# Two softmax attentions whose q and k are projected densely and laid to row quadrants by transfers, with the row maxima as a ninth row, halved weighted sums, and FP4 blocks three at a time

## The chip, the cores and the metric

The kernel runs on one core of one Trainium2 chip. A core has five engines that run side by side and wait for one another by semaphores: TensorE (PE, matrix products; loading its weights is listed apart as PEld), VectorE (DVE), ScalarE (ACT), GpSimd (POOL) and SyncE (SP, which issues transfers). PE writes to PSUM only. The metric is the device time of one execution, in microseconds.

## The reference, cut to what matters

The model is a chain of four layers, each of the form feed-forward, attention, feed-forward. The activations are 4 batches of 1024 tokens of width 128, all in float32. The change touches the feed-forward and the attention of layer 0, the attention of layer 1, and one detail of the expert layers.

- Layer 0, feed-forward (run before and after its attention): inputs and weights are quantized to FP4 in blocks of 16 values (scale = largest magnitude / 6), then gate and up projections of width 352, silu times up, quantized again, and a down projection.
- Layer 0, attention: 16 heads of 8, **causal**, softmax, then an output projection, a recurrence of 8 steps with tanh, and a dense feed-forward with gelu.
- Layer 1, attention: 16 heads of 8, **not causal**, with biases.

```python
qkv = (xn @ qkv_w + qkv_b).reshape(b, s, 3, H, HD)
scores = jnp.einsum('bhqd,bhkd->bhqk', q, k) / np.sqrt(HD)
attn_w = jax.nn.softmax(scores, axis=-1)
attn = jnp.einsum('bhqk,bhkd->bhqd', attn_w, v)
```

Layers 2 and 3 (experts, two linear attentions, ternary feed-forwards) are not touched, but for the expert layers' scatter.

## The kernel before

Tokens are cut into 8 blocks of 512 (two to a batch), which stay in SBUF as `x`. Every stage is a Python generator; each `yield` is a point where another generator may put its instructions into the engines' queues. `run` advances the stage of the moment and gives each of its steps one `tick` to the side queue, in which the start of the next batch, the end of the last batch and the front of the next stage wait. `woven` runs several generators in turn. The tile framework places the instructions, adds the semaphores and finds free buffers; each engine then executes its own queue strictly in order.

**Attention (lines 552 to 717).** The 16 heads are taken in 4 groups of 4 (`NG`), for each of 4 batches: 16 groups an attention, counted `n`. PE's 128 rows are used as four quadrants of 32 rows: head `i` of a group has its 8 values of q and k in rows `32i` to `32i+7`, and the weights are padded with zeros to bring them there (`_packed_heads`). Two chains run for each group:

- `maxima` first projects q and k of the group (L591, two matmuls of 128x512 for each half of the 1024 tokens; the profile has two records for every f32 matmul), evicts them with their biases (L594 on ACT, L595 on DVE), then computes scores with queries in the partitions (L607) and reduces them over the keys on DVE, negated (L619). In the causal case a mask is added by a matmul of bf16 (L613). At the end of a group the maxima are transposed (L385) and added to q as a ninth row (L627, `qm`). That k has a one in its ninth row makes the next scores come out with the maximum subtracted.
- `weighted` computes the scores again with keys in the partitions (L653), takes the exponential on ACT (L658), masks the diagonal on POOL when causal (L661), and sums the values weighted by it (L640, four heads in four column groups of 32, so that `acc` gets 4 x 32 rows). Values carry a column of ones, so the sum of weights comes along. The sums of one chunk of keys are issued after the scores of the next. When 512 queries are done, `acc` is copied (L672), transposed, and divided by the sum of the weights (L676, L677).

`softmax_attention` weaves both: each step of `weighted` (two heads of one chunk of 128 keys) is followed by one step of the maxima of the next group; weighting of a group begins `LEAD = 4` steps after its maxima are complete. A step of the weaving is below called half a step where a whole one is a chunk of keys for four heads. Scores, accumulators and transposes share the pool `ps_one` of four PSUM buffers of 2 KB a partition; `big` has two buffers of 4 KB, for maxima and projections.

**FP4 feed-forward (lines 499 to 549).** `l0_block` handles one block of 512 tokens: layernorm, quantization (`fp4`, a chain over DVE and POOL, L460 to L473), transposes, projections (L524), silu and product, quantization again, transposes, down projection (L541) into an `acc` that the block holds from its first projection to its end. Two blocks are woven, 12 steps apart. When the second FP4 stage begins, the last batch of the attention's end (output projection, recurrence L824 and L825, gelu feed-forward) still runs from the side queue, and blocks 6 and 7 need it.

**Expert layers.** `front` routes the tokens of a chunk of blocks and scatters their rows to DRAM with indirect transfers from POOL (L1321), two for each tile of 128 tokens, with a yield after every second tile.

Of the kernel before, what the change touches and what calls it, by code (L numbers as in the profile page):

```python
# [46 lines left out]
LEAD = 4  # L47
# [3 lines left out]


def _packed_heads(w, extra=None):

    out = np.zeros((*w.shape[:-1], 32), np.float32)
    out[..., :HD] = w
    if extra is not None:
        out[..., HD] = extra
    return out
# [7 lines left out]
def _softmax_attn_weights(q, k, v, out_w, bq, bk, bv, out_b):  # L67

    ws = [
        _packed_heads(q).reshape(D, H * 32),  # L70
        _packed_heads(k).reshape(D, H * 32),
        v.reshape(D, D),
        out_w,
    ]
    vecs = [
        _columns(_packed_heads(bq).reshape(-1)),

        _columns(_packed_heads(bk, 1.0).reshape(-1)),
        _columns(out_b),
    ]  # L80
    return np.concatenate(ws, 1), np.concatenate(vecs, 1), np.tile(bv.reshape(1, D), (P, 1))
# [123 lines left out]
class _Kernel:  # L205
# [5 lines left out]
    def __init__(self, ctx, tc, ins, out):  # L211
# [3 lines left out]
        self.mix = ctx.enter_context(tc.tile_pool(name="mix", bufs=2))  # L215

# [213 lines left out]
    def opened(self, name, side):  # L430

        stack = ExitStack()
        pool = stack.enter_context(self.tc.tile_pool(name=name, bufs=2, side=side, reuse_waits="tile"))

        def close():
            stack.close()
            return
            yield

        return pool, close  # L440
# [60 lines left out]
    def l0_ffn(self, side):  # L501
        pool, close = self.opened("l0f", side)
        done = self.follow
        yield from woven((self.l0_block(pool, blk, done) for blk in range(NBLK)), 2, 12)
        finish(close())
# [46 lines left out]
    def attention_tiles(self, pool):  # L552

        self.mxs = [pool.tile([P, NT, 4, 32], F32, tag=f"mx{k}", name=f"mx{k}", bufs=1) for k in range(2)]
        for t in self.mxs:
            self.nc.gpsimd.memset(t, 0.0)
        self.vas = [pool.tile([P, NT, VW], F32, tag=f"va{k}", name=f"va{k}", bufs=1) for k in range(2)]
        for t in self.vas:
# [21 lines left out]
    def maxima(self, pool, out, mx, xnT, g, wqk, vecs, causal):  # L580

        nc = self.nc
        qT = pool.tile([P, S], F32, tag="qT", name="qT", bufs=2)
        kT = pool.tile([P, S], F32, tag="kT", name="kT", bufs=3)
        for half in range(S // BLK):
            cols = bass.ts(half, BLK)
            ps = self.big()
            for j in range(2):  # L590
                nc.tensor.matmul(  # L591
                    ps[:, j, :], lhsT=wqk[:, bass.ts(j * NG + g, P)], rhs=xnT[:, cols], start=True, stop=True
                )
            nc.scalar.activation(qT[:, cols], ps[:, 0, :], AF.Identity, bias=vecs[:, g : g + 1])  # L594
            nc.vector.tensor_scalar(kT[:, cols], ps[:, 1, :], vecs[:, NG + g : NG + g + 1], None, ALU.add)  # L595
        part = pool.tile([P, NT, 2, 4], F32, tag="part", name="part", bufs=2)
        for t in range(NT):
            n = (t + 1) * P if causal else S
            for c in range(0, n, BLK):
                w = min(n - c, BLK)  # L600
                diag = causal and c + w == n
                for pair in range(2):
                    heads = (2 * pair, 2 * pair + 1)
                    ps = self.big()
                    for j, i in enumerate(heads):
                        rows = slice(32 * i, 32 * i + 32)
                        nc.tensor.matmul(  # L607
                            ps[:, j, :w], lhsT=qT[rows, bass.ts(t, P)], rhs=kT[rows, c : c + w],
# [7 lines left out]
                    to = part[:, t, c // BLK, 2 * pair : 2 * pair + 2]  # L616
                    if n <= BLK:
                        to = mx[:, t, 2 * pair : 2 * pair + 2, HD]
                    nc.vector.tensor_reduce(to, ps[:, :, :w], AX.X, ALU.max, negate=True)  # L619
                    yield  # L620
        first = TPB if causal else 0
# [841 lines left out]
```

## Time and profile before

| what | time |
|---|---|
| median of 3 runs | 5242.22 us (5237.9 to 5248.3) |
| the profiled execution | 5245.33 us |
| its span, first to last instruction | 5243.6 us |
| mean granted TensorE clock | 0.893 |
| busy: PE, DVE, ACT, POOL | 4429.8, 2539.3, 1714.6, 1040.5 us |

By start and end of the lines named, the stages are: first FP4 feed-forward to about 235 us; causal attention from there to 1286, when its last accumulator is copied; second FP4 feed-forward, with the end of the last batch, to 1623; routing and experts of layer 1; attention of layer 1 from 1979 to 3265; the rest, which the change leaves alone, to 5243.6. PE's busy time covers matmuls whose ends are modelled and which overlap, so it is not a measure of how full the array is. What an engine waits for is put down to the last semaphore that released it.

### The profile page before, as it was taken

The page shows a single profiled execution, that of the slowest core. Times are in us where ns is not written, and L with a number is a line of the kernel's source. Part 1 is how long each engine was busy: PE and PEld are TensorE (multiplying, and loading weights), DVE is VectorE, ACT ScalarE, POOL GpSimd, SP SyncE. Part 2 cuts the span into 40 slices and gives each one's busy share as a digit, 9 for nine tenths or more (in the row PEclk, how much of TensorE's full clock was granted, in tenths as well). Part 3 has the DMA queues.
Part 4 walks back from the last instruction along what each step waited for, and adds up shares of the span by engine and source line. Part 5 has one row for each costly group of instructions (what it writes and reads, how often), then busy time and mean ns, then how long its engine had stood idle before and what let it go on. Part 6 is the DMA issues. An engine that isn't in the chain of part 4 may idle for free. (4 is left out here: it accounts for less than half of the span.)

```text
span 5243.6 us, 51536 instructions
## 1 busy us (share of the span) xinstructions
PE 4429.8 (84%) x19588; PEld 1969.4 (38%) x19588; DVE 2539.3 (48%) x5415; ACT 1714.6 (33%) x3016; POOL 1040.5 (20%) x1403
## 2 busy tenths in 40 slices
PE   4799999998743987999988998695596859699899
PEld 3533333333432442333333332342243534244544
DVE  8666766573853336666655663333313721321510
ACT  1134443443211221554544545121232423122322
POOL 4211111111343014000010010104514241500000
PEclk8699999998865996999999999897797879799999
DMA  2000000000000320000000000231132013100000
GB/s 88 0 1 1 1 1 1 1 1 1 1 16 36 118 96 29 1 1 1 1 12 5 1 13 1 94 115 60 35 134 77 34 66 137 44 0 0 1 8 8
DMA packets 68090, 162.91 MB, mean 31 GB/s; under 512 B 13739, under 2 KB 22443, under 8 KB 67075
## 3 DMA queue, kind: packets, MB, share of 16 engines
q0 software_dynamic: 29632, 93.89, 5.3%
q1 hardware_dynamic: 38211, 65.73, 3.7%
q8 instruction: 155, 2.54, 0.2%
q14 instruction: 92, 0.75, 0.0%
HBM read 110.54 MB, written 49.02 MB: 30 GB/s over the span
## 5 line engine op out<-in xcount | busy, mean ns | idle before, releaser
L658 ACT ACTIVATE es<-sc 128x512 f32<-128x512 f32 (+3 forms) x1792 | 883.3, 553 | 976.2 <-PE sc L653 588.9
L653 PE MATMUL sc<-qm,kT 32*128 32x512 f32 (+3 forms) x3584 | 1090.4, 602 | 19.1 <-ACT es L658 17.6
L619 DVE TENSOR_REDUCE part<-big 128x2 f32<-128x1024 f32 (+3 forms) x768 | 880.9, 1156 | 432.6 <-PE big L607 299.5
L607 PE MATMUL big<-kT,qT 32*128 32x512 f32 (+3 forms) x3584 | 1015.9, 630 | 41.6 <-DVE part L619 27.3
L653 PEld LDWEIGHTS sc<-qm,kT 32*128 32x128 f32 x3584 | 380.9, 188 | 653.4 <-ACT es L658 398.7
L1355 PE MATMUL big<-xT,w 128*128 128x512 f32 x1104 | 520.7, 602 | 2.7 <-ACT xT L1406 2.7
L372 POOL TENSOR_TENSOR ln_rs<-ln_ve,neg_half 128x4 f32<-128x4 f32 x120 | 126.7, 1057 | 1665.2 <-DVE ln_ve L371 1661.4
L1207 PE MATMUL big<-h,l3f_w 128*128 128x512 f32 x1024 | 445.6, 596 | 4.6 <-DVE h L1193 3.2
L640 PE MATMUL acc<-es,va 128*32 128x512 f32 (+3 forms) x3584 | 446.7, 578 | 2.4 <-issue 2.3
L607 PEld LDWEIGHTS big<-kT,qT 32*128 32x128 f32 x3584 | 297.2, 193 | 177.2 <-DVE part L619 103.2
L1348 PE MATMUL acc<-h,w 128*128 128x512 f32 x736 | 361.2, 593 | 1.1 <-DVE h L1359 1.1
L1355 PEld LDWEIGHTS big<-xT,w 128*128 128x128 f32 x1104 | 209.3, 193 | 250.0 <-issue 245.7
L661 POOL TENSOR_SCALAR_AFFINE_SELECT es<-es 128x128 f32<-128x128 f32 x512 | 162.5, 327 | 702.7 <-ACT es L658 694.1
L1321 POOL DMA_INDIRECT rows_in<-xn,rows x256 | 248.8, 972 | 261.3 <-DVE p_to L1010 140.0
L1207 PEld LDWEIGHTS big<-h,l3f_w 128*128 128x128 f32 x1024 | 194.4, 191 | 251.1 <-issue 241.7
L1039 POOL DMA_INDIRECT y<-rows_out,rows x256 | 250.9, 980 | 188.7 <-DMA rows_out<-yr 88.6
L1359 DVE TENSOR_TENSOR h<-h,big 128x512 f32<-128x512 f32 x184 | 126.6, 688 | 319.3 <-ACT h L1358 319.3
L375 DVE TENSOR_SCALAR xn<-x,ln_mv,ln_rs 128x128 f32<-128x128 f32 x352 | 115.8, 380 | 308.7 <-PE tr L385 108.6
L385 PE MATMUL tr<-ident,fp_q 128*88 128x128 f32 (+1 forms) x324 | 74.8, 395 | 185.1 <-POOL fp_q L473 185.1
L1358 ACT ACTIVATE h<-big 128x512 f32<-128x512 f32 x184 | 109.9, 597 | 324.8 <-PE big L1355 324.8
L1363 ACT ACTIVATE h<-big 128x1024 f32<-128x1024 f32 x124 | 126.9, 1024 | 246.7 <-PE big L1355 193.7
L385 PE MATMUL tr<-ident,xn 128*128 128x128 f32 x288 | 59.9, 329 | 165.7 <-issue 115.6
(277 smaller groups left out, 5038.9 us busy)
## 6 DMA issues: line engine op xcount, KB each, us to landing
xr<-rows_in SPq DMA_DIRECT2D x92, 256.0 KB, 2.6
rows_out<-yr SPq DMA_DIRECT2D x92, 256.0 KB, 2.0
rows_in<-zero SPq DMA_DIRECT2D x5, 1024.0 KB, 7.6
rows_in<-xn,rows POOLq DMA_INDIRECT x256
y<-rows_out,rows POOLq DMA_INDIRECT x256
l3f_w<-in_l3f_w SPq DMA_DIRECT2D x1, 2816.0 KB
x<-in_x SPq DMA_DIRECT2D x8, 256.0 KB, 5.9
out<-x SPq DMA_DIRECT2D x8, 256.0 KB, 2.3
```

The costliest lines, as they stand in the source:

```text
L385: self.nc.tensor.transpose(ps[:n, i * P : (i + 1) * P], t, self.ident)
L607: nc.tensor.matmul(ps[:, j, :w], lhsT=qT[rows, bass.ts(t, P)], rhs=kT[rows, c : c + w], start=True, stop=not diag,)
L619: nc.vector.tensor_reduce(to, ps[:, :, :w], AX.X, ALU.max, negate=True)
L640: nc.tensor.matmul(out[32 * i : 32 * i + 32, off:], lhsT=va[:, kc, (4 * g + i) * (HD + 1) :][:, :32], rhs=es[i][:, off:], start=kc == 0, s ...
L653: nc.tensor.matmul(ps[:, off:], lhsT=kT[rows, bass.ts(kc, P)], rhs=qm[rows, qb * BLK + off : (qb + 1) * BLK], start=True, stop=True,)
L658: nc.scalar.activation(es[i][:, off:], ps[:, off:], AF.Exp, scale=ISQ)
L661: nc.gpsimd.affine_select(out=block, in_=block, compare_op=ALU.is_ge, fill=0.0, base=0, pattern=[[1, P]], channel_multiplier=-1,)
L1039: nc.gpsimd.indirect_dma_start(out=y, out_offset=None, in_=self.rows_out[:, :], in_offset=bass.IndirectOffsetOnAxis(ap=rows[:, k, t : t + ...
L1207: nc.tensor.matmul(ps[:, j, :], lhsT=m[:, i * FF + (2 * pair + j) * P : i * FF + (2 * pair + j + 1) * P], rhs=hs[z][:, i, :], start=i == 0 ...
L1321: put = nc.gpsimd.indirect_dma_start(out=k.rows_in[:, :], out_offset=bass.IndirectOffsetOnAxis(ap=self.rows[:, i, first + t : first + t + ...
L1348: nc.tensor.matmul(out, lhsT=w[:, (2 if gated else 1) * FF + c * D :][:, :D], rhs=h, start=c == 0, stop=c == NC - 1)
L1355: nc.tensor.matmul(ps[:, j, :], lhsT=w[:, bass.ts(col, P)], rhs=xT, start=True, stop=True)
```

## The change

Dense projection: the weights of q and k are no longer padded. `dense` projects all 16 heads of a batch at once (two matmuls of 128x512 for each half), and `laid_out` copies, for each group, the 8 partitions of each head's q and k to a quadrant with four transfers on SP, into one of three tiles `qks`, a group ahead of its maxima. `qks` was filled with ones, so that row 8 of k is one.

Maxima: they are finished for each half of the queries; one transpose brings the 4 heads x 4 tiles to 16 rows, which are copied, written to DRAM and read back as four rows of 512, each to row 8 of q in its quadrant. `maxima` contracts 8 rows, the second scores 9. Weighting of a half starts 6 steps after its maxima (`LEAD`).

Sums: `summed` cuts the sums of a chunk into two halves of 256 queries (the first chunk is done in one), and `along` issues one after each step. Copying, transposing and dividing an accumulator (`divided`) is likewise spread over the following steps. The exponentials get ten buffers for nine.

FP4: three blocks are woven, 8 steps apart, with three buffers for each tile. Scatter: `front` yields after every tile.

```diff
-LEAD = 4
+LEAD = 6
+QKS = 3
...
+    ws = [q.reshape(D, D), k.reshape(D, D), v.reshape(D, D), out_w]
+    vecs = [_columns(b.reshape(-1)) for b in (bq, bk, out_b)]
...
+        self.memory = ctx.enter_context(tc.tile_pool(name="memory", bufs=1, space=bass.MemoryType.DRAM))
...
-        pool, close = self.opened("l0f", side)
+        pool, close = self.opened("l0f", side, bufs=3)
         done = self.follow
-        yield from woven((self.l0_block(pool, blk, done) for blk in range(NBLK)), 2, 12)
+        yield from woven((self.l0_block(pool, blk, done) for blk in range(NBLK)), 3, 8)
         finish(close())
...
-        self.mxs = [pool.tile([P, NT, 4, 32], F32, tag=f"mx{k}", name=f"mx{k}", bufs=1) for k in range(2)]
-        for t in self.mxs:
-            self.nc.gpsimd.memset(t, 0.0)
+
+        self.qks = [pool.tile([P, 2, S], F32, tag=f"qk{k}", name=f"qk{k}", bufs=1) for k in range(QKS)]
         self.vas = [pool.tile([P, NT, VW], F32, tag=f"va{k}", name=f"va{k}", bufs=1) for k in range(2)]
-        for t in self.vas:
+        for t in self.qks + self.vas:
             self.nc.gpsimd.memset(t, 1.0)
...
+    def dense(self, qd, xnT, w, vecs):
 
         nc = self.nc
-        qT = pool.tile([P, S], F32, tag="qT", name="qT", bufs=2)
-        kT = pool.tile([P, S], F32, tag="kT", name="kT", bufs=3)
         for half in range(S // BLK):
             cols = bass.ts(half, BLK)
             ps = self.big()
             for j in range(2):
-                nc.tensor.matmul(
-                    ps[:, j, :], lhsT=wqk[:, bass.ts(j * NG + g, P)], rhs=xnT[:, cols], start=True, stop=True
-                )
-            nc.scalar.activation(qT[:, cols], ps[:, 0, :], AF.Identity, bias=vecs[:, g : g + 1])
-            nc.vector.tensor_scalar(kT[:, cols], ps[:, 1, :], vecs[:, NG + g : NG + g + 1], None, ALU.add)
-        part = pool.tile([P, NT, 2, 4], F32, tag="part", name="part", bufs=2)
-        for t in range(NT):
-            n = (t + 1) * P if causal else S
-            for c in range(0, n, BLK):
-                w = min(n - c, BLK)
-                diag = causal and c + w == n
+                nc.tensor.matmul(ps[:, j, :], lhsT=w[:, bass.ts(j, D)], rhs=xnT[:, cols], start=True, stop=True)
+            nc.scalar.activation(qd[:, 0, cols], ps[:, 0, :], AF.Identity, bias=vecs[:, 0:1])
+            nc.vector.tensor_scalar(qd[:, 1, cols], ps[:, 1, :], vecs[:, 1:2], None, ALU.add)
+            yield
+
+    def laid_out(self, n, qd):
+
+        for i in range(4):
+            at = (n % NG * 4 + i) * HD
+            self.nc.sync.dma_start(out=self.qks[n % QKS][32 * i : 32 * i + HD], in_=qd[at : at + HD])
...
+    def maxima(self, pool, n, qb, causal):
+
+
+        nc = self.nc
+        qk = self.qks[n % QKS]
+        one = causal and qb == 0
+        mx = pool.tile([P, 4, TPB], F32, tag="mx", name="mx", bufs=2)
+        part = None if one else pool.tile([P, 2, 4, TPB], F32, tag="part", name="part", bufs=2)
+        for t in range(TPB):
...
-                            ps[:, j, :w], lhsT=qT[rows, bass.ts(t, P)], rhs=kT[rows, c : c + w],
+                            ps[:, j, :w], lhsT=qk[rows, 0, bass.ts(q, P)], rhs=qk[rows, 1, c : c + w],
...
-        first = TPB if causal else 0
-        nc.vector.tensor_tensor(mx[:, first:, :, HD], part[:, first:, 0, :], part[:, first:, 1, :], ALU.min)
-        qm = pool.tile([P, S], F32, tag="qm", name="qm", bufs=2)
-        for half in range(S // BLK):
-            ps = self.transposed([mx[:, half * TPB + i].rearrange("p h r -> p (h r)") for i in range(TPB)])
-            cols = bass.ts(half, BLK)
-            nc.vector.tensor_tensor(qm[:, cols], ps, qT[:, cols], ALU.add)
-        out += [kT, qm]
-
-    def weighted(self, pool, at, va, g, kT, qm, causal):
+        if not one:
+            nc.vector.tensor_tensor(mx, part[:, 0], part[:, 1], ALU.min)
+        ps = self.tr()
+        m = 4 * TPB
+        nc.tensor.transpose(ps[:m, :P], mx.rearrange("p i t -> p (i t)"), self.ident)
+        rows = pool.tile([m, P], F32, tag="mrows", name="mrows", bufs=2)
+        nc.vector.tensor_copy(rows, ps[:m, :P])
+        by = self.memory.tile([4, BLK], F32, tag="mrows", name="mrows", bufs=4)
+        nc.sync.dma_start(out=by.rearrange("i (t q) -> (i t) q", q=P), in_=rows)
+        for i in range(4):
+            at = 32 * i + HD
+            nc.sync.dma_start(out=qk[at : at + 1, 0, bass.ts(qb, BLK)], in_=by[i : i + 1, :])
...
+
+            def steps():
+                yield from begin(b, xnT)
+                yield from self.dense(qds[b], xnT, w, vecs)
+                if b == 0:
+                    self.laid_out(0, qds[b])
+                yield from self.values(self.vas[b % 2], xnT, wv, bv)
+
+            starts[b] = steps()
+            self.side.append(starts[b])
+
+        def all_maxima():
+            nonlocal steps
+            start(0)
+            finish(starts.pop(0))
+            for n in range(B * NG):
+                b, g = divmod(n, NG)
+                if g == 1 and b + 1 < B:
+                    start(b + 1)
+                if n + 1 < B * NG:
+                    if g == NG - 1:
+                        finish(starts.pop(b + 1))
+                    self.laid_out(n + 1, qds[(n + 1) // NG])
+                for qb in range(nqb):
+                    for _ in self.maxima(pool, n, qb, causal):
+                        steps += 1
+                        yield
+                    done[n, qb] = steps
+
...
+        def summed(n, kc, es, off, out, last):
+
+            b, g = divmod(n, NG)
+
+            def half(k):
+                if kc == 0 and k == 0:
+                    out.append(self.acc())
+                lo, hi = max(off, k * BLK // 2), (k + 1) * BLK // 2
+                if kc == 0:
+                    lo, hi = off, BLK * (1 - k)
+                for i in range(4 if lo < hi else 0):
                     nc.tensor.matmul(
-                        out[32 * i : 32 * i + 32, off:], lhsT=va[:, kc, (4 * g + i) * (HD + 1) :][:, :32],
-                        rhs=es[i][:, off:], start=kc == 0, stop=last,
+                        out[0][32 * i : 32 * i + 32, lo:hi],
+                        lhsT=self.vas[b % 2][:, kc, (4 * g + i) * (HD + 1) :][:, :32],
+                        rhs=es[i][:, lo:hi], start=kc == 0, stop=last and k == 1,
                     )
 
-            for kc in range(nk):
-                diag = causal and kc >= qb * TPB
-                off = (kc - qb * TPB) * P if diag else 0
-                es = [None] * 4
-                for pair in (1, 0):
-                    for i in (2 * pair, 2 * pair + 1):
-                        rows = slice(32 * i, 32 * i + 32)
-                        ps = self.one("sc")
-                        nc.tensor.matmul(
-                            ps[:, off:], lhsT=kT[rows, bass.ts(kc, P)],
-                            rhs=qm[rows, qb * BLK + off : (qb + 1) * BLK], start=True, stop=True,
-                        )
-                        es[i] = pool.tile([P, BLK], F32, tag="es", name="es", bufs=9)
-                        nc.scalar.activation(es[i][:, off:], ps[:, off:], AF.Exp, scale=ISQ)
-                        if diag:
-                            block = es[i][:, off : off + P]
-                            nc.gpsimd.affine_select(
-                                out=block, in_=block, compare_op=ALU.is_ge, fill=0.0, base=0,
-                                pattern=[[1, P]], channel_multiplier=-1,
-                            )
-                    yield
-                if waiting:
-                    values(*waiting)
-                waiting = (kc, es, off, out, kc == nk - 1)
-            values(*waiting)
-            waiting = None
+            return [lambda k=k: half(k) for k in range(2)]
...
             un = pool.tile([P, BLK], F32, tag="un", name="un", bufs=2)
-            nc.vector.tensor_copy(un, out)
+            nc.vector.tensor_copy(un, out[0])
+            yield
...
+        def along():
+
+            if tails and next(tails[0], tails) is tails:
+                tails.popleft()
+            if pending:
+                pending.popleft()()
+            while pending and not callable(pending[0]):
+                tails.append(pending.popleft())
...
+            for qb in range(nqb):
+                while (n, qb) not in done or steps < done[n, qb] + LEAD:
+                    if next(maxima, maxima) is maxima:
+                        break
+                    yield
+                qk, out = self.qks[n % QKS], []
+                nk = (qb + 1) * TPB if causal else NT
+                for kc in range(nk):
+                    diag = causal and kc >= qb * TPB
+                    off = (kc - qb * TPB) * P if diag else 0
+                    es = [None] * 4
+                    for pair in (1, 0):
+                        for i in (2 * pair, 2 * pair + 1):
+                            rows = slice(32 * i, 32 * i + HD + 1)
+                            ps = self.one("sc")
+                            nc.tensor.matmul(
+                                ps[:, off:], lhsT=qk[rows, 1, bass.ts(kc, P)],
+                                rhs=qk[rows, 0, qb * BLK + off : (qb + 1) * BLK], start=True, stop=True,
+                            )
+                            es[i] = pool.tile([P, BLK], F32, tag="es", name="es", bufs=10)
+                            nc.scalar.activation(es[i][:, off:], ps[:, off:], AF.Exp, scale=ISQ)
+                            if diag:
+                                block = es[i][:, off : off + P]
+                                nc.gpsimd.affine_select(
+                                    out=block, in_=block, compare_op=ALU.is_ge, fill=0.0, base=0,
+                                    pattern=[[1, P]], channel_multiplier=-1,
+                                )
+                        next(maxima, None)
+                        along()
+                        yield
+                    pending.extend(summed(n, kc, es, off, out, kc == nk - 1))
+                pending.append(divided(n, qb, out))
...
-            if t % 2:
-                yield
+            yield
```

## The prediction

> **What bounds the kernel now.** I first cut the span into stages, with the table of busy time by stretch (columns: stretch, length, then busy time and instructions of PE, PEld, DVE, ACT, POOL, granted clock, DMA share, GB/s). The change touches the four FP4/attention stretches at the front and the second attention.
>
> ```profile
> 36.00:235.00 199.00, 130.23 (x549) 99.84 (x548) 145.00 (x363) 38.66 (x73) 76.19 (x61) 0.72 0.00 1
> 300.00:1286.00 986.00, 943.29 (x5780) 360.76 (x5778) 602.10 (x991) 433.10 (x895) 184.46 (x527) 0.93 0.00 1
> 1286.00:1440.00 154.00, 107.46 (x366) 61.37 (x367) 125.88 (x308) 42.78 (x65) 48.51 (x38) 0.81 0.00 1
> 1440.00:1623.00 183.00, 94.91 (x432) 75.84 (x430) 109.77 (x335) 30.57 (x54) 80.67 (x70) 0.65 0.03 12
> 2080.00:3265.00 1185.00, 1129.37 (x6572) 391.75 (x6572) 708.07 (x906) 584.79 (x1079) 54.38 (x56) 0.97 0.01 4
> ```
>
> The two attentions (rows 2 and 5) have PE busy for 95%, DVE for 60%, ACT for 45 to 50%. The FP4 stretches have DVE busy for 60 to 82%. What a busy PE means in an attention shows in the timeline of one step of the non-causal one: one chunk of 128 keys against 512 queries.
>
> ```profile
> 2421.85 0.19 PEld L653 LDWEIGHTS sc<-qm,kT 32*128 32x128 f32 x2 [0.84 <-ACT es L658]
> 2421.86 0.70 PE L653 MATMUL sc<-qm,kT 32*128 32x512 f32 x2
> 2421.87 0.70 PE L607 MATMUL big<-kT,qT 32*128 32x512 f32 x2
> ...
> 2422.83 1.52 PE L653 MATMUL sc<-qm,kT 32*128 32x512 f32 x3
> 2423.01 1.57 ACT L658 ACTIVATE es<-sc 128x512 f32<-128x512 f32 x3 [1.46 <-PE big L607]
> ...
> 2423.66 0.18 PEld L653 LDWEIGHTS sc<-qm,kT 32*128 32x128 f32 x1 [0.64 <-ACT es L658]
> 2423.67 0.70 PE L607 MATMUL big<-kT,qT 32*128 32x512 f32 x2
> ...
> 2424.72 0.16 PEld L640 LDWEIGHTS acc<-es,va 128*32 128x32 f32 x8 [0.76 <-issue]
> ...
> 2425.72 0.70 PE L653 MATMUL sc<-qm,kT 32*128 32x512 f32 x2
> ```
>
> Every f32 matmul is two records, one per pass. Two score matmuls (L653) and two of the maxima (L607) sit in four row quadrants and run together: 0.98 us from 2421.85 to 2422.83. Then a third score runs alone, because the fourth waits for the first exponential (L658) to give back its PSUM buffer: the pool has four, one of them the accumulator. So the next four-fold block starts at 2423.66, not 2422.83: 0.83 us late. It takes 1.05, the weighted sums (L640) 1.00, and the step 3.87. The wait for that exponential is what the change can win.
>
> How much of a stage is such steps, is read from the copies of the finished accumulator (L672, two to a group of four heads):
>
> ```profile
> L672 DVE COPY un<-acc x7: 691/692/692, 307.1 to 447.6; 128x512 f32<-128x512 f32 x7
> L672 DVE COPY un<-acc x5: 691/692/693, 2113.4 to 2250.4; 128x512 f32<-128x512 f32 x5
> ```
>
> Undisturbed groups take (447.6-307.1)/3 = 46.8 us in the causal attention (12 steps) and (2250.4-2113.4)/2 = 68.5 us in the other: 16 steps of 3.87 = 61.9, and 6.6 around them. Most of the 6.6 is where the next group's q and k are made:
>
> ```profile
> 2430.65 1.41 PE L385 MATMUL tr<-ident,mx 128*128 128x128 f32 x8
> 2431.89 3.60 PE L591 MATMUL big<-xnT,l1a_w 128*128 128x512 f32 x8
> 2435.42 1.13 PE L607 MATMUL big<-kT,qT 32*128 32x512 f32 x4
> ```
>
> **Part 1: sums in halves.** The order becomes [two scores, two maxima], half of the sums (256 columns), and again. The half goes where the PE waited. Its price: the L640 block takes 0.996 us at 512 columns and 0.783 at 384 (from its start to the next block's), so 0.143 fixed and 0.427 per 256: 0.57 for a half, 1.14 instead of 1.00 for a step. In one half-step from t: four-fold block 1.05, half 0.57, so the next could start at t+1.62. But its second score needs the exponential of this one's first score, free at t+1.81 (2421.85 to 2423.66). With h the half-step, the block starts at max(0, 1.81-h) after its turn: h = 1.81-h+1.62, h = 1.715, a step 3.43. Saved 0.44 of 3.87. DVE needs 2 x 1.22 of it and ACT 4 x 0.52, so neither takes over. The exponentials are ready for their half: the last of a half-step starts near t+1.66 and ends at t+2.26; its sums come at t+2.77.
>
> A rule of the Trainium skill speaks against this ("TensorEngine Tiling (Array Packing)", Key Properties): changing the tiling mode drains the array. Scores use 32x128 tiles and sums 128x32, so the changes go from 2 to 4 a step. It gives no figure. By the row, a sums block pays 0.143 for both its changes, which is in the 0.57. Were it 0.31 more, h would be 1.62+0.31 = 1.93, the step as long as before, and the whole sum below 93 instead of 234 (rival a). I take the row.
>
> **Part 2: one dense projection a batch.** L591 goes from 64 matmuls an attention to 16. A group loses 3.6 us of L591 and gets back 0.9 as its share. It also loses the waits for kT, 0.76 and 0.47 us in the stretch shown. Four copies on SP per group (8 partitions x 8 KB) spread q and k to the quadrants, a whole group ahead; hidden except before the first group (2.0 us, the median landing of the row below). Scores now contract 9 rows and maxima 8, not 32; the time of a matmul here follows its columns, so I cost that at nothing, and bound it in the rivals.
>
> **Part 3: the maxima as ninth row.** Eight transposes (1.41 us) and two additions go; each half of the queries gets one transpose of 8 columns wide maxima, a copy, one SP transfer to DRAM and four back. PE executes in order, so that transpose stands at the head of PE until the last reduction is done: from the block's start 1.24 to the reduction (L619), 1.22 for it, 0.2 for the minimum (estimate, from the DVE operations on 32 columns), ready at 2.7; the maxima block queued behind would have started at 1.72; with 0.3 for the transpose 1.3 late. Behind it wait that block, the sums and so ACT. 2.6 a group. The transfers:
>
> ```profile
> xr<-rows_in SPq DMA_DIRECT2D x92, 256.0 KB, 2.6
> rows_out<-yr SPq DMA_DIRECT2D x92, 256.0 KB, 2.0
> ...
> l1a_w<-in_l1a_w SPq DMA_DIRECT2D x1, 640.0 KB, 7.0
> ```
>
> Rows ready at 3.3 us after the last block began; issue 0.4, landing 2.0, four issues of 0.45 (the spacing of SP's issues at the start of the program), landing 2.6: 10.1. The first score that needs the row comes six half-steps later: 1.72+1.3+6 x 1.715 = 13.3. Hidden, with 3.2 to spare. SP carries nothing else in an attention. In the causal one those six are narrow (blocks of 128 to 384), some 9 us, and about 1 is left; I cost it at nothing, up to 2 us a group.
>
> **Part 4: the end of an accumulator.** Old and new accumulators and a transpose buffer then share four PSUM buffers. One score waits for the copy: 1.24+1.22+0.69 = 3.15 after the block, where 2.04 was due (1.1 late), and four transposes (0.66) follow. 1.7 each, 3.4 a group. Before, spacings of 31.4 us for eight steps leave 0.44.
>
> **Sum of the attentions.** Non-causal, a group: 16 x 3.43 = 54.9, plus 2.6+3.4+0.9 = 6.9: 61.8 for 68.5, so 6.7 x 16 = 107. Weighting starts after 22 blocks of maxima instead of 36; these run at half clock there, 1.74 each: 24, less 2 for the first copies. Together 129. Causal, a group: four full steps 1.8; the eight masked steps between +0.14 and -0.44 each, taken as 0, because there masks and PE set the pace already; projection 3.9; maxima +1.2, accumulators +1.0. 3.5 x 16 = 56, and 4 for the start (22 blocks of maxima alone instead of 28, most of them narrow, less the first copies): 60.
>
> **Part 5: FP4 by three.** Two blocks in flight leave DVE idle for 54 of 199 us. A third fills that, but each block holds a PSUM accumulator, so one of four buffers is left for the transposes. The skill's page "SBUF — State Buffer" (SBUF: two separate sides) says that GpSimd and a VectorE operation of two SBUF inputs or a two-port mode lock each other out. Counting all DVE so, 145+76 = 221 would exceed 199 and nothing would be won; the trace overlaps them in part, yet one mask of 704 columns (L469) took 1.69 us where its mean is 0.66, beside a POOL operation. Between 0 and 45 us I take 15. In the second FP4 stage (1286 to 1623) the recurrence of the last batch takes the first 154 us; from the built order 3.6 blocks instead of 3.0 are done by its end. 0.6 blocks at 36 us is 22, plus some 25 from the rest at three in flight, less the routing of three blocks, which moves behind the last one (24 scatters at 1.27): between -10 and +75, taken as 30. The scatters' finer yield moves nothing by itself.
>
> 129+60+15+30 = 234. The profiled run took 5245.3 (span 5243.6), the median is 5242.2; so **5008 us**.
>
> **Rivals.** (a) The halves win nothing, because the drain or the buffers eat it: 0.44 x (256+64) steps = 141 are lost, 5150. For it: four buffers stay four. Against: the wait is there at each step. (b) More is won: boundaries of 6.0 a group fall to 2 (64), masked steps gain 0.44 too (56), FP4 becomes DVE-bound (45): 4845. For it: spare time on all other engines. (c) Slower: the row of maxima comes late. Chain 5.5 plus two landings against 13.3, 64 times. It decides from 3.66 us late each (234/64), that is landings of 5.7. At the 7.0 that a loaded queue shows above, 6.2 x 64 = 397 is lost: 5405. Against: those landings were at 318 GB/s, the attentions move 1 to 4. (d) The change doesn't do what it says: nine-row operands don't share the array. Then each half-step is some 0.85 longer, over 5500; the built instructions keep tiles of 32x128, so it holds 0.02, within (c)'s side.
>
> **How the numbers follow.** Forecast 0.57 (own range 4890 to 5110), (a) 0.19, (b) 0.12, (c) and (d) 0.10, no change 0.02. Changes under 0.2% can't be told from none. Faster 0.57+0.19+0.12 = 0.88. The range 4815 to 5195 holds the forecast, (a) and (b).
>
> **What would show it.** Score steps 3.4 us apart; the fourth score's wait at 0.1 instead of 0.64; L591's successor with 32 records an attention; transposes of maxima with PE waiting about 1 us for DVE; no score waiting for a DMA; first FP4 stage under 190 us. Wrong if scores wait for DMA, if a step stays at 3.8, or if the two scores of a pair no longer overlap.

## The result and the profile after

The changed kernel takes **6099.9 us** (6083.6 to 6112.3, four runs) against 5245.3 before (5237.9 to 5248.5, four runs): ratio **1.163, interval 1.159 to 1.167**. The forecast was 5008. The profiled run's span is 6110.3 us, 867 more than before's 5243.6.

The busy time by stretch (columns as in the prediction; the number before the DMA share is the granted clock). Rows 2 and 5 run from the first to the last accumulator copy of an attention, rows 3 and 4 are the second FP4 stage, cut after the same 154 us. Row 1 has the prediction's times; the last block of the first FP4 stage ends only after it, at 263 us (231.5 before).

```profile
36.00:235.00 199.00, 112.03 (x455) 83.48 (x454) 135.81 (x324) 33.64 (x62) 67.50 (x51) 0.70 0.00 0
335.00:1616.00 1281.00, 1252.16 (x6397) 412.41 (x6397) 586.46 (x985) 419.46 (x866) 183.67 (x519) 0.63 0.02 4
1616.00:1770.00 154.00, 103.81 (x377) 62.36 (x377) 130.37 (x296) 37.45 (x61) 44.42 (x33) 0.78 0.00 1
1770.00:1916.00 146.00, 83.67 (x378) 64.69 (x379) 104.15 (x311) 30.03 (x51) 68.06 (x60) 0.71 0.03 10
2448.00:4120.00 1672.00, 1644.44 (x7978) 436.47 (x7977) 681.14 (x913) 555.53 (x1019) 56.44 (x58) 0.52 0.02 5
```

Between the first and the last accumulator copy the two attentions now last 1277 and 1671 us. Before, the same copies were 979 and 1151 us apart. That is 298 and 520 us more, 818 of the 867. PE is busy for 98% of both, as it was for 95%, but the granted clock is 0.63 and 0.52 where it was 0.93 and 0.97. DVE and ACT do no more work than before.

The timeline of one half-step of the non-causal attention (start, duration, engine, line, operation):

```profile
3560.34 1.08 PE L682 MATMUL acc<-es,va 128*32 128x256 f32 x8
3561.35 1.22 PE L741 MATMUL sc<-qk 9*128 9x512 f32 x2
3561.36 1.22 PE L598 MATMUL big<-qk 8*128 8x512 f32 x2
3562.36 1.06 PE L741 MATMUL sc<-qk 9*128 9x512 f32 x2
3562.38 1.06 PE L598 MATMUL big<-qk 8*128 8x512 f32 x2
3563.37 1.08 PE L682 MATMUL acc<-es,va 128*32 128x256 f32 x8
```

The order is the one that the change writes, and the scores and maxima still start together in four quadrants. But a four-fold block takes 2.02 us (3561.35 to 3563.37), where the prediction has 1.05, and half of the sums 1.01 (3560.34 to 3561.35), where it has 0.57. A half-step is 3.03 us instead of 1.715. The sums contract 128 rows as before and are slower by the same factor as the scores: it is not the short matmul that is slow, but PE's clock. The copies of the accumulator show it over whole groups:

```profile
L693 DVE COPY un<-acc x4: 681/681/681, 2498.4 to 2654.1; 128x512 f32<-128x512 f32 x4
L693 DVE COPY un<-acc x5: 681/681/681, 400.4 to 545.2; 128x512 f32<-128x512 f32 x5
```

Three spacings in the first line give (2654.1-2498.4)/3 = 51.9 us, so 103.8 for a non-causal group (68.5 before, 61.8 forecast). The second holds two causal groups of 72.4 (46.8 before, 43.3 forecast). In the list of waits no score waits for a transfer; one block of maxima does, once, for the first q and k (12.6 us).

### The profile page after: what moved, and what is told of

Same layout as the page of the kernel before. It is cut to its first block, busy times and chain, and to the rows that moved or that the text cites. A ratio compares the mean times of both kernels' runs of the same rounds, so it can differ in the third digit from the quotient of the medians.

```text
span 6110.3 us, 57033 instructions
## 1 busy us (share of the span) xinstructions
PE 5288.9 (87%) x21764; PEld 2073.1 (34%) x21764; DVE 2515.8 (41%) x5383; ACT 1690.2 (28%) x2966; POOL 1051.1 (17%) x1405
## 5 line engine op out<-in xcount | busy, mean ns | idle before, releaser
L741 PE MATMUL sc<-qk 9*128 9x512 f32 (+3 forms) x3584 | 1630.1, 980 | 27.9 <-issue 15.4
L598 PE MATMUL big<-qk 8*128 8x512 f32 (+3 forms) x3584 | 1576.3, 984 | 55.6 <-DVE part L608 33.3
L682 PE MATMUL acc<-es,va 128*32 128x256 f32 (+2 forms) x6144 | 818.1, 622 | 4.7 <-issue 1.8
L741 PEld LDWEIGHTS sc<-qk 9*128 9x128 f32 x3584 | 452.5, 289 | 701.3 <-issue 388.5
L598 PEld LDWEIGHTS big<-qk 8*128 8x128 f32 x3584 | 426.0, 289 | 102.8 <-DVE part L608 59.8
L682 PEld LDWEIGHTS acc<-es,va 128*32 128x32 f32 x6144 | 152.0, 136 | 872.5 <-issue 847.8
```

Of the source, the lines that this page charges most:

```text
L598: nc.tensor.matmul(ps[:, j, :w], lhsT=qk[rows, 0, bass.ts(q, P)], rhs=qk[rows, 1, c : c + w], start=True, stop=not diag,)
L682: nc.tensor.matmul(out[0][32 * i : 32 * i + 32, lo:hi], lhsT=self.vas[b % 2][:, kc, (4 * g + i) * (HD + 1) :][:, :32], rhs=es[i][:, lo:hi] ...
L741: nc.tensor.matmul(ps[:, off:], lhsT=qk[rows, 1, bass.ts(kc, P)], rhs=qk[rows, 0, qb * BLK + off : (qb + 1) * BLK], start=True, stop=True,)
```

## The experiments

The theory after this reading: the clock follows how many of the array's 128 rows are at work. A four-fold block has 2 x 9 + 2 x 8 = 34 of them in the changed kernel and 128 before. The rivals: the order of the halves costs the clock, or the clock is lost before the attentions and does not come back.

The record names three chips. The kernel before has a median of 5142 us on the one that ran e1 to e4, 5143 on that of e5 to e8, and 5244 on that of e9 to e11, near the 5245 of the result. Ratios are to the kernel before on the same chip. e2 is compared below with e6 and e7 across the first two, which differ by 1 us.

**e1: the kernel before, with the rows alone changed.** The first slice is that of the maxima, the second that of the scores. The rows left out hold zeros, so nothing of the result changes; e3 and e8 do the same with 16 and 24 rows in both.

```diff
-                        rows = slice(32 * i, 32 * i + 32)
+                        rows = slice(32 * i, 32 * i + HD)
-                            rows = slice(32 * i, 32 * i + 32)
+                            rows = slice(32 * i, 32 * i + HD + 1)
```

> The kernel before, with one thing changed: its score matmuls contract 9 rows and its maxima 8, not 32 (the rows left out hold zeros, so the result is the same). Theory (rows): the granted clock of TensorE follows how many rows of the array are at work, and 4 x 8 of 128 are too few; both attentions then run at a clock near 0.5 with the old order, no transfers and whole sums. A step is then two blocks of 2.0 us, one of 2.0 with a lone score, and sums of 2.0: about 7 for 3.87, so 6300 to 6600 us. Rival 1 (order): the halved sums double the changes of tiling mode, and the drained array reads as idle; then this kernel stays at 5245 and a clock of 0.89. Rival 2 (history): the clock is lost at the start of the attention, after FP4 by three or by the earlier weighting; then 5245 too.

Measured: 6122.3 us (one run) beside 5142.2 for the kernel before, less than the 6300 to 6600 expected. Two slices cost 980 us; order, transfers, DVE and ACT work are those of the kernel before. Its timeline and a stretch of undisturbed groups:

```profile
2562.72 1.94 PE L640 MATMUL acc<-es,va 128*32 128x512 f32 x8
2564.58 1.22 PE L653 MATMUL sc<-qm,kT 9*128 9x512 f32 x2
```

```profile
2500.00:2610.00 110.00, 110.00 (x412) 35.24 (x416) 44.56 (x43) 37.30 (x66) 0.00 (x0) 0.55 0.00 1
```

The sums, which the edit does not touch, take 1.86 us to the next block's start instead of 1.00. PE is busy for every microsecond of this stretch and gets a clock of 0.55. Both rivals fall: neither the order nor the start of the attention differs from before.

**e2: the changed kernel, with 32 rows.** The tiles are filled so that the rows past the ninth add nothing (q is 0, k is 1); four more SP transfers a group clear the row in which q meets the maxima's row.

```diff
-        for t in self.qks + self.vas:
+        for t in self.qks:
+            self.nc.gpsimd.memset(t[:, 0, :], 0.0)
+            self.nc.gpsimd.memset(t[:, 1, :], 1.0)
...
+            row = 32 * i + HD
+            self.nc.sync.dma_start(out=self.qks[n % QKS][row : row + 1, 0, :], in_=self.none)
...
-                        rows = slice(32 * (2 * pair + j), 32 * (2 * pair + j) + HD)
+                        rows = slice(32 * (2 * pair + j), 32 * (2 * pair + j) + 32)
...
-                            rows = slice(32 * i, 32 * i + HD + 1)
+                            rows = slice(32 * i, 32 * i + 32)
```

> The kernel after, with 32 rows contracted in both products: q is zero in the rows that are added, k one, and four more transfers a group clear the maxima's row of q before its maxima. All else as in the kernel after: halves, transfers, FP4 by three. Theory (rows): the clock of the attentions is back at 0.93 to 0.97 and the forecast's own sum can be read: about 5010 us, a step of 3.43 us. Rivals 1 and 2 (order, history): nothing changes, 6100 us and a clock of 0.70.

Measured: 5031.9 us, ratio **0.979 (0.974 to 0.984)**: with the rows back, the change is faster than the kernel before. Multiplications by zero are enough to hold the clock. Its timeline, copies, and a stretch of undisturbed groups:

```profile
2440.04 0.64 PE L689 MATMUL acc<-es,va 128*32 128x256 f32 x8
2440.61 0.70 PE L748 MATMUL sc<-qk 32*128 32x512 f32 x2
...
2441.68 0.64 PE L689 MATMUL acc<-es,va 128*32 128x256 f32 x8
...
2443.54 0.64 PE L689 MATMUL acc<-es,va 128*32 128x256 f32 x8
...
2447.04 0.64 PE L689 MATMUL acc<-es,va 128*32 128x256 f32 x8
```

```profile
L700 DVE COPY un<-acc x5: 678/680/681, 2128.5 to 2249.1; 128x512 f32<-128x512 f32 x5
```

```profile
2120.00:2180.00 60.00, 59.84 (x506) 19.92 (x506) 41.89 (x42) 34.75 (x64) 0.00 (x0) 1.00 0.05 6
```

The step is 3.50 us (2440.04 to 2443.54 to 2447.04), half of the sums 0.57, a group 2 x (2249.1-2128.5)/4 = 60.3, the clock 1.00.

**e3, e4, e8: how many rows it takes.** e4 is the changed kernel with 32 rows in the scores and 8 in the maxima.

> The kernel before with 16 rows contracted in scores and maxima: 64 of 128 rows when four quadrants run. Theory (rows): it tells on which side of the bound half the array lies. With a clock near 0.5: 6300 to 6600 us; with 0.89: 5245. Anything between would say that the clock of a stretch mixes. Rivals 1 and 2: 5245.

> The kernel after with 32 rows in the scores alone, 8 in the maxima: 64 + 16 = 80 of 128 rows in a block of four. Theory (rows): faster than the 6100 of the kernel after if what counts is the sum of active rows; near 6100 if each matmul has to fill its quadrant. Rivals 1 and 2: 6100.

> The kernel before with matmuls over 24 rows of each quadrant instead of 32 (the rows left out hold zeros, so nothing of the result changes). Nine rows gave 6122 us at a granted clock of 0.72, sixteen 5886 at 0.76, thirty-two 5142 at 0.89. If the clock follows the rows at work in proportion, 24 lies between: some 5500 at 0.83. If there is a level above which the clock is given in full, 24 is either at 5150 or at some 5800.

One run each for e1, e3, e4 and e8; the changed kernel's row is from the result, on a slower chip:

```
kernel                       rows of 128 in a four-fold block   us      non-causal group, us
e1: before, 9 and 8 rows      34                                6122.3  108 to 114
after, 9 and 8 rows           34                                6099.9  103.8
e3: before, 16 rows           64                                5886.4  101 to 106
e4: after, 32 and 8 rows      80                                5565.3  60.1 or 103.8
e8: before, 24 rows           96                                5264.8  68.5
before, 32 rows              128                                5142    68.5
e2: after, 32 rows           128                                5031.9  60.3
```

It is no proportion: between 64 and 96 rows the clock changes over, and e4 stands on the edge. e3 lies between its two expected answers because its clock switches within a group: 1.00 from 2800 to 2810 us of its trace, 0.50 from 2820 to 2850. Two stretches of e4's non-causal attention, in which the same loop runs, and then the end of the first kind and what follows it:

```profile
2800.00:2900.00 100.00, 99.76 (x855) 32.96 (x847) 70.62 (x71) 58.23 (x108) 0.00 (x0) 1.00 0.04 7
3345.00:3445.00 100.00, 100.00 (x494) 24.69 (x494) 40.80 (x40) 33.65 (x62) 0.00 (x0) 0.50 0.00 1
...
2912.00:2922.00 10.00, 7.37 (x50) 2.41 (x43) 9.07 (x25) 4.96 (x9) 1.01 (x1) 1.00 0.00 0
2930.00:3060.00 130.00, 130.00 (x634) 37.34 (x638) 59.64 (x108) 42.86 (x80) 30.83 (x32) 0.50 0.07 19
```

The clock is whole in one and half in the other, for 100 us each, and its groups are 60.1 us (e2's) or 103.8 (the changed kernel's). The clock falls after ten microseconds in which PE was busy for only 7.37, and stays down for 130 with PE busy throughout. Three of the other four falls in this attention also follow such a lull (6.95 to 8.51 of 10 us), one does not; what brings the clock back was not settled. The 24 rows of e8 hold the clock in undisturbed groups and lose it in the last one, which has scores and no maxima beside them. Here is an inner group, then the last one, then the last one of the kernel before:

```profile
2250.00:2318.00 68.00, 67.91 (x409) 23.15 (x408) 43.95 (x43) 35.70 (x66) 0.00 (x0) 1.00 0.00 1
3219.00:3321.00 102.00, 91.88 (x268) 22.32 (x264) 2.84 (x7) 34.33 (x64) 0.00 (x0) 0.52 0.00 0
...
3203.00:3264.00 61.00, 51.43 (x264) 14.47 (x264) 2.40 (x6) 34.12 (x64) 0.00 (x0) 1.00 0.00 1
```

That group lasts 101.4 us instead of 61.6. Of e8's two expectations, 24 in proportion at some 5500 or a level at 5150, the result is nearer the level, 122 us above before's median: 40 of them are this group, and 38 lie in the causal attention (1016.9 us between its first and last accumulator copy, 978.9 before).

**e5: the FP4 blocks by three, alone in the kernel before.**

```diff
-        pool, close = self.opened("l0f", side)
+        pool, close = self.opened("l0f", side, bufs=3)
-        yield from woven((self.l0_block(pool, blk, done) for blk in range(NBLK)), 2, 12)
+        yield from woven((self.l0_block(pool, blk, done) for blk in range(NBLK)), 3, 8)
```

> The kernel before with one part of the change alone: the FP4 blocks of the first layer woven by three, eight steps apart, in pools of three buffers. The theory of the prediction: both FP4 stages gain, 15 us in the first and 30 in the second, so 45 of some 5142 on this chip, ratio 0.991. The rival, read from the changed kernel's trace (first stage 263 us instead of 231, second 300 instead of 337): three in flight lose some 20 to 30 in the first stage, gain 37 in the second, ratio 0.996 to 0.999. If the first stage ends at 231 or earlier here, its loss in the changed kernel belongs to another part (the new tiles or the start of the attention), not to the weaving.

Measured: 5174.7 us, ratio **1.006 (1.005 to 1.008)**, slower by 32 where 45 were to be gained, and outside the rival's range too. The last block of the first stage ends (x<-acc) 20 us later than before:

```profile
L547 DVE SCALAR_TENSOR_TENSOR x<-acc,x x8: 683/692/692, 88.4 to 251.6; 128x512 f32<-128x512 f32 x8
```

Before, that line reads 71.1 to 231.5. Groups of DVE between 60 and 200 us, first of the kernel before, then of e5 (columns: count, busy us, mean ns, idle before and its releaser), and one line of e5's waits there:

```profile
L472 DVE SCALAR_TENSOR_TENSOR fp_w<-fp_e,fp_w 128x704 f32<-128x704 f32 (+1 forms) x15 | 12.3, 818 | 0.0
L470 DVE TENSOR_SCALAR fp_e<-fp_e 128x704 f32<-128x704 f32 (+1 forms) x15 | 7.3, 489 | 0.1
```

```profile
L472 DVE SCALAR_TENSOR_TENSOR fp_w<-fp_e,fp_w 128x704 f32<-128x704 f32 (+1 forms) x14 | 14.7, 1049 | 0.1
L470 DVE TENSOR_SCALAR fp_e<-fp_e 128x704 f32<-128x704 f32 (+1 forms) x13 | 10.4, 800 | 0.1
```

```profile
DVE x L547 <- PE acc L541: 30.6, 4, 8.3
```

The means are 28% and 64% longer with a third block in flight, and DVE shows 144.6 us busy of 199 (145.0 before), for 343 instructions instead of 363. But the medians hardly move (879 ns for 862, 514 for 520): a few operations are very long. Two of them in e5's timeline, with the POOL operations beside them, and one that has none:

```profile
127.08 1.61 POOL L465 TENSOR_TENSOR fp_y<-h,fp_inv 128x704 f32<-128x704 f32 x1 [0.19 <-DVE fp_inv L464]
127.49 1.59 DVE L470 TENSOR_SCALAR fp_e<-fp_e 128x704 f32<-128x704 f32 x1
...
130.24 0.51 DVE L470 TENSOR_SCALAR fp_e<-fp_e 128x704 f32<-128x704 f32 x1
...
131.63 1.97 POOL L473 TENSOR_TENSOR fp_q<-fp_w,fp_scale 128x704 f32<-128x704 f32 x1 [2.93 <-DVE fp_w L472]
132.39 1.96 DVE L472 SCALAR_TENSOR_TENSOR fp_w<-fp_e,fp_w 128x704 f32<-128x704 f32 x1
```

The first ends 0.39 us after its POOL operation (129.08 and 128.69), the other 0.75 (134.35 and 133.60). All nine operations of L470 to L472 that are long in this stretch start 0.41 to 0.76 us after a POOL operation and end about 0.4 (L470) or 0.75 us (the others) after its end; before, none of the three lines has a long one there. What looks like use of the idle time is waiting inside the instructions, some 9 us over the medians in these nine (an estimate from their durations). And DVE stands for 30.6 us in four waits at the last operation of a block, which needs PE's sums; this wait is not in the list before.

The second stage does gain. From the last causal accumulator to the last block's end e5 takes 276 us, where the 24-row kernel, by two on the same chip, takes 339; but the first accumulator of the next attention comes only 22 us sooner (804.6 us instead of 826.7). So the stages about cancel in the traces, and where the median's loss of 32 lies is open: the unchanged kernel has no trace from that chip.

**e6 and e7: the changed kernel with 32 rows, with one part undone.** e6 weaves the FP4 blocks by two again; e7 makes the sums whole:

```diff
-            return [lambda k=k: half(k) for k in range(2)]
+            return [lambda: None, whole]
```

> The changed kernel with 32 rows, and the FP4 blocks woven by two again, twelve steps apart. If three in flight are worth the 45 us of the prediction, this is slower than the 32-row kernel by about that (ratio to before 0.988 for 0.979). If they lose 21 in the first stage and gain 37 in the second, it is some 16 slower (0.982). If the first stage's loss was the whole of it, it is faster (0.975).

> The changed kernel with 32 rows, and the weighted sums whole again (512 columns in one piece, after the second half of the following key step, as in the kernel before). The prediction's part 1: the halves are worth 0.44 us in each of 320 steps, 141 us, so this is at some 5170 (ratio to before 1.006 for 0.979), and an undisturbed non-causal group is 60.2 + 16 x 0.44 = 67.2 us. Rival (a) of the prediction, halves that win nothing: the group stays near 60 and the ratio near 0.98.

Measured: e6 5017.6 us, ratio 0.976 (0.974 to 0.977); e7 5027.6, ratio 0.977 (0.976 to 0.979). By three costs 14 us of the medians here, which the overlapping intervals don't make certain; in the traces the first FP4 stage ends at 252.3 us by three (e2) and at 230.3 by two (e6). The halves, forecast at 141, show **no gain**. e7's timeline of a step and its copies:

```profile
2441.65 1.07 PE L686 MATMUL acc<-es,va 128*32 128x512 f32 x8
...
2444.45 0.18 PEld L745 LDWEIGHTS sc<-qk 32*128 32x128 f32 x1 [0.64 <-ACT es L750]
...
2445.51 1.07 PE L686 MATMUL acc<-es,va 128*32 128x512 f32 x8
```

```profile
L697 DVE COPY un<-acc x5: 680/681/681, 2095.0 to 2219.3; 128x512 f32<-128x512 f32 x5
```

The wait for the exponential (0.64) is back and the step is 3.86, so the halves do win 0.36 a step, 5.8 a group. But e7's group is 2 x (2219.3-2095.0)/4 = 62.2 and not 66.1: 16 x 3.86 = 61.8 and 0.4 for everything else, against 16 x 3.50 = 56.0 and 4.3 in e2. The ends of the accumulators and the maxima's transposes lie in the wait for the exponential while there is one, and come to light when it goes. From the first accumulator copy to the last, the non-causal attention takes 1006 us in e2 and 1029 in e7, so the halves gain 23 there. In the causal attention they lose: e7 takes 915 us, e2 956 and e6 949. Part of it is in the last group, 49.7 us in e6 and 35.1 in e7. The stretches of it, e6 first:

```profile
1205.00:1255.00 50.00, 47.71 (x239) 15.06 (x237) 3.17 (x10) 18.90 (x44) 7.97 (x28) 0.61 0.00 1
```

```profile
1217.00:1252.00 35.00, 29.23 (x191) 9.76 (x189) 3.10 (x9) 18.67 (x44) 7.97 (x28) 0.99 0.01 2
```

In this group, which has no maxima beside the scores, the clock is 0.61 with halves and 0.99 with whole sums. Why is open: in the kernel before it is 0.67 in the same group with whole sums, and in e2's last non-causal group it is 1.00 with halves. The rest of the 34 to 42 us lies in groups that side work disturbs, and no run singles out its cause.

**e9, e10, e11: the parts together.** e9 is the kernel before unchanged, for its stages on the chip at hand. e10 is e2 with both undone: the dense projection and the ninth row are left. e11 puts each part where it gained: sums whole in the causal attention and in halves in the other, FP4 by two in the first stage and by three in the second.

> The kernel before, unchanged, for its stages on the chip that ran the experiments: its median here is 5142 us, and 5245 on the chip of the first comparison. Expected: undisturbed groups as there (46.8 and 68.5 us), the first accumulator copy at 318 us, and the 100 us of difference in the stages with many transfers and in the disturbed groups (the groups that the feed-forward work of the next layer runs beside). From the 24-row kernel, which shares them: 827 us between the last accumulator of the causal attention and the first of the other, some 1090 for the non-causal attention, 1931 after it.

> The 32-row kernel with both the FP4 blocks by two and the sums whole: of the change, only the dense projection and the maxima as a ninth row are left. Added up from the single edits: first accumulator copy at 317 us, 915 for the causal attention, 812 to the next, 1029 for the other, 1934 after it: 5007, ratio to before 0.974. If the two edits do not add, it is off this by more than 10 us. By the prediction's sizes for what is left (a non-causal group 61.8 + 16 x 0.44 = 68.8, so nothing gained there) it would be at 5142 - 80, ratio 0.984 or more.

> The 32-row kernel with each part where it gained: sums whole in the causal attention and in halves in the other, FP4 blocks by two in the first stage and by three in the second. From the stages of the runs before: 317 + 915 + 806 + 1005 + 1932 = 4975 us, ratio to before 0.968, the fastest so far. If the stages are not independent, it stays near the 0.9756 of the 32-row kernel with blocks by two.

These three ran on the slower chip, so e9 (5247.6 us) repeats before's own trace: undisturbed groups of 46.8 and 68.5. The stages of the faster chips were therefore not had from it. e10: 5116.8 beside 5243.9, ratio **0.975 (0.972 to 0.979)**, at its expected 0.974. e11: 5078.9, ratio **0.968 (0.964 to 0.971)**, also as expected, and the lowest ratio of all.

## Why the prediction was wrong

**The step that failed** is in part 2: "Scores now contract 9 rows and maxima 8, not 32; the time of a matmul here follows its columns, so I cost that at nothing". By e1 it costs 980 us in the kernel before. By ratios it costs 1.163 - 0.979 = 0.184 of 5245 in the changed one, 965 us. A matmul's time follows its columns at a given clock, and the rows decide the clock.

The warning stood in the trace of before, in a number that the prediction used without asking why: blocks of maxima alone "run at half clock there". The prediction says so of the start of the non-causal attention; the start of the causal one shows the same with PE fuller:

```profile
248.00:285.00 37.00, 35.58 (x105) 12.40 (x102) 24.71 (x48) 0.00 (x0) 3.02 (x3) 0.50 0.00 0
```

PE is busy for 96% of it and gets 0.50. A block of maxima takes two of the four quadrants, 64 rows; now and then two blocks overlap, and the masks use all rows. PE busy and clock at half is a contradiction as long as one takes busy time for activity. The Trainium skill ("TensorE: Matmul & The Clock Gate", Part 1) invites that: it ties the gate to how busy PE has been and asks for no long gaps in PE's work. It also says that the gate, apart from a limiter for several busy cores, has two settings only, and e4 agrees (0.50 and 1.00). But busy time does not tell them apart here: 100% busy holds 1.00 with 128 rows and 0.55 with 34 (e2, e1). The measurement decides.

The other parts, with the clock restored; of the 234 us forecast, e2 has 110 (5142.2 - 5031.9):

- **What bounds the kernel**, PE's order in the attentions: right. Giving PE's clock away cost all that it did because PE was the bound.
- **Part 1, halves.** The step was right: 3.43 forecast, 3.50 measured. The mode change that the skill's tiling rule warns of costs no more than the row said: half of the sums takes 0.57. The worth was wrong: 141 forecast, none measured (5031.9 with halves, 5027.6 without). The failed step is the assumption that the boundaries of a group add to its steps in both cases; with whole sums all but 0.4 of them is hidden in the wait that the halves remove. That leaves the 23 us of the non-causal attention, and the causal one loses more. Rival (a) had the size, and not the reason: neither drain nor buffers ate the gain of a step; its number came out by luck.
- **Parts 2 to 4, projection, ninth row, accumulator ends.** The forecast leaves them 234 - 141 - 45 = 48 us; e10 gives 127 (5243.9 - 5116.8). Between the accumulator copies of e9 and e10, 69 of them are in the non-causal attention and 57 in the causal one, where 16 and 32 were forecast. The mis-sized term in the non-causal one is the same boundary: 6.9 a group at half sums, measured 4.3, and 0.4 at whole ones. A non-causal group came to 60.3 (61.8 forecast), a causal one to 42.7 (43.3). The row of maxima arrives in time, so rival (c) falls.
- **Part 5, FP4 by three.** Forecast a gain of 45, measured a loss of 32 in the kernel before, and no gain in the 32-row kernel (14 slower, within the intervals). "A third fills that" failed: the third block lengthens the others' operations and brings its own wait. The rule that the prediction weighed and set aside ("SBUF — State Buffer", two separate sides: GpSimd and some VectorE operations lock each other out) had its sign right, and the trace agrees with it: the long operations of L470 to L472 end about 0.4 or 0.75 us after the POOL operation that runs when they start. How the 20 us of the first stage divide between this and the wait for PE's sums is open. In the second stage, e2 leads e6 by 7 us from the last causal accumulator to the first of the next attention, and e5 the 24-row kernel by 22, where 30 were forecast; the forecast's own terms (22 + 25 - 30) make 17.
- **Rival (d)** stood over 5500 and held 0.02, so its side came true. Its mechanism did not: nine-row operands do share the array, and every block is slow because of the clock.

## What to carry to other kernels

Read the granted clock beside PE's busy time, and count rows: a matmul that packs four quadrants should fill all their 32 rows, with zeros if need be, since rows that add nothing were worth 18% of this kernel. Before a wait is removed, ask what else hides in it; a step that is 0.36 us faster was worth 2 us of 5.8 in a group, and nothing in the end. Compare the longest execution of an operation with its median: DVE operations that took two or three times theirs were waiting inside for POOL, and a third block in flight made more of these waits.

## What the hardware showed that was not expected

- PE at 100% busy stays at about half clock (0.50 to 0.59) with 34 or 64 of 128 rows at work in its four-fold blocks, and at 1.00 with 96 or 128 in undisturbed groups, though the sums between them always use all 128. With 80 rows it holds either, for 100 us at a time.
- Rows of zeros count: the 32-row kernels multiply zeros in 23 or 24 rows of each quadrant and keep the clock.
- The whole PE slows, not the short matmuls alone: half of the sums went from 0.57 to 1.01 us.
- Chips differ by 2% on the kernel before: medians of 5142, 5143 and 5244 us. e5, which leaves the attentions of before as they are, has on its chip the same causal attention (978.8 us between its copies, 978.9 in before's trace), but 1103.7 instead of 1151.0 in the non-causal one and 1941 instead of 1979 us after it. Undisturbed groups are equal (46.8 and 68.5); the cause is not known.
